# Register loads a block ahead, late sums behind the gelu, a later router and moved bias copies in a fused MoE and recurrent kernel

## The chip, the cores and the metric

The kernel runs on one core of a Trainium2 chip. The metric is the device time of one execution in microseconds (us). Before the change three runs gave 2498.42, 2498.41 and 2495.82 us, median 2498.41. The engines are named as the profile names them: PE is TensorE's matmul stream, PEld its weight loads, DVE is VectorE, ACT is ScalarE, POOL is GpSimd, SP is SyncE (which here only issues DMAs). PEq, DVEq, ACTq and so on are the sequencers of these engines: register operations, register loads, branches and DMA issues run there.

## What is computed

The reference puts two layers one behind the other over 32 sequences of 128 tokens with 512 features, all in float32. Cut to its core:

```python
# layer 0, mixture of 8 small experts, two for each token, and a shared expert
shared = (silu(x @ sw1.T) * (x @ sw3.T)) @ sw2.T
s      = sigmoid(x @ router_w.T + (cond @ router_t_w.T)[:, None, :])
top2   = top_k(s + router_bias, 2)            # gates: s of the two, normalised
routed = sum over the two of gate * (gelu(x @ rw1[e].T) @ rw2[e].T)
h0     = (shared + routed) / 3
# one of 8 large experts for each whole sequence, chosen by its last token
sel    = argmax(softmax(gelu(h0[:, -1] @ Wp1 + bp1) @ Wp2 + bp2))
x      = x + h0 + 0.3 * ((gelu(h0 @ W1[sel] + b1[sel]) @ W2[sel] + b2[sel]) @ Wo + bo)
# layer 1, 16 experts chosen by a hash of the token, with a capacity; then a recurrence
y      = sigmoid(xr @ w_recept.T) * (square(relu(expert_in @ w_key)) @ w_value)[slot]
c      = sigmoid(y@wf.T + c@uf.T + bf) * c + sigmoid(y@wi.T + ...) * tanh(y@wc.T + ...)
x      = x + tanh(y @ wo.T + c_final @ uo.T + bo)
```

## The kernel before

Each float32 operand of a large matmul is cut into a high part (a cast to a reduced float32, on ACT, L64) and the remainder (a subtraction, on DVE, L65); `split` does this, and `mm3` (L82) makes three matmuls of each pair of pieces: high by high, high by low, low by high. So every tile that a matmul reads goes through ACT and then DVE.

The work comes in stages. The 32 sequences are 8 groups of 4 (512 tokens each).

1. **Shared expert, groups 0 to 3** (to about 303 us). `shared` runs over 8 chunks of hidden features for each group: two times 12 matmuls up (`p`), and 12 down into four accumulators (`acc`), a chunk behind. One chunk takes some 10 us at the start. `hook2` puts small work between the chunks. In group 0, `mid0` also spreads the *router* through the chunks: for each group and each of four feature pieces, `fetch_r` loads a piece of x (`xr`), and `router` splits it and adds two matmuls to the scores `rt`, which lie in the only buffer of the PSUM pool `ps_r`; after four pieces ACT copies them to `zt` (L397). `cut` says which pieces belong to which half chunk. The raw pieces of the router, of x and of the weights share one pool of six buffers, and all are loaded over SP's queue. `seq_bias` makes the part of the scores that belongs to the sequence (`ps_tb`): four products on DVE, each then summed over the partitions by a float32 matmul of 256 columns. Its call stands under `if n + w == 1`, which is true for chunk 0, second half, and for chunk 1, first half. After that, `choose` makes the two experts of each token, the list of tokens of each *block* (`blk_t`), the expert of each block (`blk_e`, as a column offset into the weights) and the number of blocks in use (`used_i`). `slots` does the like for layer 1.

2. **Routed experts** (303 to 548 us). A block is 128 token slots of one expert; there are 64 blocks that are always full enough to run and up to seven more (64 to 70). The loop over `i` does for one block: `r_up` (12 matmuls `pur` with the weights at a column that a register holds, then a gelu on ACT into `ge`), `turn_x` for block i+1 (four transposes `ptx`, then the split into `xb`), `take` for block i+3 (POOL's gather), `r_down` for block i-1 (6 matmuls `por` with a register's column, a copy on DVE, a store over SP), and `turn_h` (2 transposes `pth` and a split into `hbr`). The register is loaded by `first_col` (L663) on TensorE, inside `r_up`, and pinned behind the last `pur` of the block before. The blocks beyond 64 come in pairs inside the loop, `maybe` (L702): their registers are loaded first, and then a branch on `used` decides whether they run; `used` is loaded into registers of four engines at i = 12 (L728).

3. **Shared expert, groups 4 to 7**, with the *sums* of the tokens' shared and routed parts between the chunks: `get_o` (two gathers on POOL, L777, and loads of `shc` and `xc` over SP, L784 and L787) and `combine` (two DVE operations, L793 and L794, four transposes `pth`, an ACT scale, stores).

4. **The large expert by sequence** (about 827 to 1430 us). The loop over `b` runs for one sequence at a time: `up` ("a" and "b" halves), `bend` (transposes, gelu with a bias, split into `hb`), `down` (`po`), and for pairs of sequences the output product `pb` and the mixes of layer 1. `used()` splits the next weights, which come by gathers on POOL (`fetch_w`, L906). The biases of the gelu come from `bias_d`, a copy in DRAM that three small-piece DMAs make (L770); the text has them behind the routed blocks, but the scheduler has SP issue them at 3.6, 17.5 and 18.1 us. The sums of the last four sequences, 28 to 31, are done inside this loop: `get_o` at b = 3, 6, 9, 12, `combine` two steps later, and `policy` at b = 17.

5. **Layer 1's experts** (`phD`, `poD`), and 6. **the recurrence** with the output (`ps_f`, `ps_i`, `ps_c`, `poF`) run to the end.

What sets the order: each engine runs its instructions in one order, but this order is not the text's. The compiler's scheduler orders the instructions of all engines by its own estimate, and may move those that depend on nothing unfinished ahead. `tc.issue_after(x)` forbids it to put what stands under it ahead of instruction `x`, and `behind(both)` does that for two instructions. DMA issues take their place in the order of the engine that issues them.

Of the kernel before, what the change touches and what calls it, by code (L numbers as in the profile page):

```python
# [49 lines left out]
def tile_kernel(ctx: ExitStack, tc: tile.TileContext, a: dict, out: bass.AP):  # L50
# [107 lines left out]
    with ExitStack() as sa:  # L158
# [6 lines left out]
        def fetch(src, name):  # L165
            t = raw_p.tile([P, D], F32, tag="raw", name=name)
            nc.sync.dma_start(out=t, in_=src)
            return t

# [35 lines left out]
        def fetch_x(g):  # L205
            if g < NG:
                x_raw[g] = [fetch(a["x"][g][:, k, :], f"xraw_{g}_{k}") for k in range(KD)]
# [68 lines left out]
        with ExitStack() as s0:  # L276
# [32 lines left out]
            fetch_sw(1)  # L309
            ps_acc = s0.enter_context(tc.tile_pool(name="ps_acc0", bufs=4, space=PSUM, **kw))  # L310
# [51 lines left out]
            def seq_bias():  # L362

                ps = ps_r.tile([P, NB, E0], F32, tag="r", name="ps_tb")
                for k in range(KD):
                    pr = rtile([P, NB, E0], f"pr_{k}")
                    nc.vector.tensor_tensor(
                        pr,
                        condT[:, k, :].unsqueeze(2).to_broadcast([P, NB, E0]),
                        rtw[:, k, :].unsqueeze(1).to_broadcast([P, NB, E0]),  # L370
                        ALU.mult,
                    )
                    mm(ps, ones, pr, k == 0, k == KD - 1)
                nc.vector.tensor_copy(tbias, ps)
# [3 lines left out]
            def fetch_r(i):  # L378
                g, k = divmod(i, KD)
                if 0 < g < NG:  # L380
                    xrs[i] = fetch(a["x"][g][:, k, :], f"xr_{g}_{k}")
# [211 lines left out]
            def cut(m):  # L593
                return min(NR, KD + (NR - KD) * (m - 1) // 15) if m > 0 else 0

            def mid0(n, w):

                if n < KF:
                    m = 2 * n + w
                    for i in range(cut(m), cut(m + 1)):  # L600
                        router(i)
                    for i in range(cut(m + 1), cut(m + 2)):
                        fetch_r(i)
                    if n + w == 1:
                        seq_bias()
# [3 lines left out]
            def hook2(g, c):  # L609

                if g == 0:
                    next(steps[0], None)
                    return
                if g == 1 or (g == 2 and c < 5):
                    for _ in range(1):
                        if next(steps[0], 0) == 0:
                            next(steps[1], None)
                    if g == 2 and c == 4:
                        for st in steps:
                            for _ in st:  # L620
# [34 lines left out]
        with s1:  # L655
# [9 lines left out]
            def r_up(i, e=None):  # L665
                if e is None:
                    with tc.issue_after(last_up[0]) if last_up else nullcontext():
                        e = first_col(i)
                x = xb.pop(i)
# [30 lines left out]
            def maybe(n):  # L700
                es = [first_col(i) for i in pairs[n]]
                with tc.If(used > pairs[n][0]):  # L702
                    for i, e in zip(pairs[n], es):
                        r_up(i, e)
# [8 lines left out]

            for i in range(NFULL + 1):
                if i < NFULL:
                    r_up(i)
                    if i + 1 < NFULL:
                        turn_x(i + 1, bx, "xb")
# [4 lines left out]
                if i < NFULL:  # L723
                    turn_h(i)
                n, step = divmod(i - FIRST, STEP)
                if i == FIRST - 4:
                    engines = (nc.tensor, nc.scalar, nc.vector, nc.sync)
                    used = nc.values_load(  # L728
                        used_i[0:1, 0:1], engines=[x.engine for x in engines], min_val=NFULL, max_val=NBLK
                    )  # L730
# [38 lines left out]
        for kind, i in BIAS.items():  # L769
            nc.sync.dma_start(out=bias_d[:, bass.ts(i, KD)], in_=a[kind][:, KD * D :])  # L770
# [127 lines left out]
        raws, bcol, changed = {}, {}, {}  # L898
# [3 lines left out]
        def fetch_w(i):  # L902
            if i < len(todo):
                kind, b = order[todo[i]]
                raws[i] = wg.tile([P, WROW], F32, tag="raw", name=f"rawB_{i}")
                nc.gpsimd.indirect_dma_start(  # L906
# [3 lines left out]
                )  # L910
                if kind == "W1a":
# [95 lines left out]
    with ExitStack() as sb:  # L1007
# [35 lines left out]
        seqs, end_p = {}, None  # L1043
# [17 lines left out]
        def fetch_hid(b):  # L1061
            if b < NB:
                hid_raw[b] = lp.tile([P, KD, P], F32, tag="hid", name=f"hidB_{b}")
                nc.sync.dma_start(out=hid_raw[b].rearrange("p k q -> p (k q)"), in_=by_seq(hid_d, b))
# [156 lines left out]
        for b in range(-1, NB + 1):  # L1221
            c, j = divmod(b - 1, PB)
            if b + 1 < NB:
# [3 lines left out]
                fetch_hid(b + 3)  # L1227
            gated = b - 4 if b % 2 == 0 and 0 <= b - 4 < NB - 6 else None
# [555 lines left out]
```

## Time and profile before

The profiled execution took 2497.2 us; its span, from the first to the last instruction that the profile shows, is 2495.5 us.

| What | Value | Where it is read |
|---|---|---|
| median of three runs | 2498.41 us (2495.82 to 2498.42) | the times |
| profiled execution, span | 2497.2 us, 2495.5 us | the times, the page's head |
| mean granted TensorE clock | 0.991 | clock of the core |
| first matmul | at 6.46 us | timeline |
| PE busy in 0 to 50 us | 39.28 of 50.00 us | busy time by windows |
| PE busy in 303 to 548 us | 236.08 of 245.00 us, clock 0.99 | busy time by windows |
| PE busy in 820 to 850 us | 23.34 of 30.00 us, clock 0.89 | busy time by windows |
| DMA from SP's queue | 246.51 MB, 29.9% of 16 engines | queues |

How to read it: a row of the timeline gives start, duration, engine, line, operation, output and inputs, and in brackets how long the engine had been idle and who ended the idle time. In the list of waits the columns are the total, the number of times and the longest wait, in us. Rows marked PEq or PEldq are the sequencer's, not the matrix unit's. The ends of matmuls are modelled, so that a matmul's row overlaps the next; distances between starts are the safer measure.

### The profile page before, as it was taken

What the parts mean: (1) busy time and instruction counts of PE and PEld (TensorE: products, weight loads), DVE (VectorE), ACT (ScalarE), POOL (GpSimd) and SP (SyncE); (2) the same over time, 40 slices, a digit from 0 to 9 for tenths busy, and PEclk for the clock granted to TensorE, in tenths of its full rate; (3) what the DMA queues carried; (4) which work ended last, traced back from release to release, by engine and by line L of the source; (5) the groups of instructions that cost most, each with busy time, mean ns of one, the idle gap of its engine ahead of it and who ended that gap; (6) DMA issues with size and microseconds to landing.
All of it is one profiled execution on the core that took longest, in us unless ns stands there. A gap on an engine that the chain in (4) does not pass through costs nothing.

```text
span 2495.5 us, 36566 instructions
## 1 busy us (share of the span) xinstructions
PE 2434.5 (98%) x12932; PEld 2060.7 (83%) x12932; DVE 1326.8 (53%) x2265; ACT 1034.5 (41%) x1826; POOL 412.3 (17%) x462
## 2 busy tenths in 40 slices
PE   8999999999999899999999999999999999999996
PEld 5788888888888788888888889999978888888885
DVE  7897644456567344454454486766642333333336
ACT  4444533343224454454454376666532222222214
POOL 1000022221233233322222100000010000000003
PEclk9999999999999999999999999999999999999998
DMA  5545544457564333341342487777431111111017
GB/s 181 168 126 169 187 161 161 163 185 238 183 215 165 115 120 127 102 153 57 118 146 94 152 295 232 222 228 234 155 125 39 38 40 42 43 42 38 26 70 280
DMA packets 193402, 351.62 MB, mean 141 GB/s; under 512 B 37504, under 2 KB 72368, under 8 KB 190144
## 3 DMA queue, kind: packets, MB, share of 16 engines
q1 hardware_dynamic: 142080, 246.51, 29.9%
q0 software_dynamic: 36448, 75.95, 10.3%
q10 hardware_dynamic: 14688, 26.75, 3.0%
q8 instruction: 108, 1.77, 0.3%
q14 instruction: 78, 0.64, 0.1%
HBM read 373.94 MB, written 88.65 MB: 185 GB/s over the span
## 4 chain that ended last, share of the span: by engine, by line
PE 49%; DVE 2%; DMA 1%; ACT 0%; issue 0%; POOL 0%; SPq 0%; POOLq 0%; DVEq 0%; ACTq 0%
PE phD L82 7%; PE ps_c L82 7%; PE ps_f L82 7%; PE ps_i L82 7%; PE poD L82 7%; PE poF L82 3%; PE po L82 3%; PE pb L82 2%; PE pv L82 1%; PE ptF L1481 1%; PE ptC L1488 1%; PE ptD L1348 0%; DMA v_d<-r 0%; DMA rawD<-in_w_value_dram 0%; PE ptB L1196 0%
## 5 line engine op out<-in xcount | busy, mean ns | idle before, releaser
L65 DVE TENSOR_TENSOR wD<-rawD,wD 128x1024 fp32r<-128x1024 f32 x128 | 156.4, 1229 | 80.8 <-ACT wD L64 80.7
L82 PE MATMUL p<-xhl,swu 128*128 128x512 f32 x768 | 188.7, 397 | 6.5 <-ACT xhl L64 6.5
L82 PE MATMUL phD<-xe,wD 128*128 128x256 f32 x1536 | 186.9, 282 | 2.0 <-DVE hf L1367 2.0
L82 PEld LDWEIGHTS phD<-xe,wD 128*128 128x128 f32 x1536 | 186.0, 190 | 3.3 <-issue 2.2
L82 PE MATMUL p<-xhl,kept_u 128*128 128x512 f32 x768 | 184.3, 394 | 0.7 <-DVE kept_u L65 0.7
L82 PE MATMUL poD<-wD,hD 128*128 128x512 f32 x768 | 181.3, 392 | 0.0
L82 PEld LDWEIGHTS p<-xhl,swu 128*128 128x128 f32 x768 | 144.6, 190 | 36.9 <-ACT xhl L64 6.5
L82 PEld LDWEIGHTS p<-xhl,kept_u 128*128 128x128 f32 x768 | 141.9, 188 | 30.0 <-DVE kept_u L65 1.1
L82 PEld LDWEIGHTS poD<-wD,hD 128*128 128x128 f32 x768 | 142.0, 188 | 28.4
L64 ACT CAST wD<-rawD 128x1024 fp32r<-128x1024 f32 x128 | 133.2, 1047 | 55.4 <-PE poD L82 50.1
L281 POOL DMA_INDIRECT xg<-in_x_rows_dram,blk_t x71 | 67.6, 952 | 454.9 <-PE ptx L291 246.4
L1456 POOL DMA_INDIRECT y<-res_d,gat_i x32 | 30.8, 962 | 573.6 <-DVE r L1476 492.1
L82 PE MATMUL pur<-r,xb 128*128 x792 | 111.5, 291 | 7.2 <-issue 4.2
L82 PE MATMUL por<-r,hbr 128*128 x396 | 108.0, 407 | 1.2 <-ACT hbr L64 1.2
L82 PEld LDWEIGHTS pur<-r,xb 128*128 128x128 f32 x792 | 99.7, 192 | 9.0 <-issue 6.9
L65 DVE TENSOR_TENSOR xb<-ptx,xb 128x512 fp32r<-128x512 f32 x68 | 47.0, 691 | 106.4 <-ACT xb L64 104.7
L82 PE MATMUL poF<-z,wo_hl 128*128 128x512 f32 x384 | 96.4, 399 | 0.0
L82 PE MATMUL ps_f<-wf_hl,z 128*128 128x512 f32 x384 | 96.2, 399 | 0.0
L82 PE MATMUL ps_c<-wc_hl,z 128*128 128x512 f32 x384 | 94.7, 396 | 0.7 <-ACT z L64 0.7
L82 PE MATMUL pb<-rT,Wo_hl 128*128 128x256 f32 x768 | 94.7, 281 | 0.3 <-DVE rT L65 0.2
L82 PE MATMUL acc<-swd,as 128*128 128x512 f32 x384 | 95.0, 392 | 0.0
L82 PE MATMUL pv<-w_recept_hl,xr 128*128 128x512 f32 x384 | 93.1, 391 | 0.5 <-ACTq L934 0.4
(1017 smaller groups left out, 4955.6 us busy)
## 6 DMA issues: line engine op xcount, KB each, us to landing
rawD<-in_w_key_dram SPq DMA_DIRECT2D x64, 512.0 KB, 4.3
rawD<-in_w_value_dram SPq DMA_DIRECT2D x64, 512.0 KB, 4.4
swr<-in_sw_dram SPq DMA_DIRECT2D x120, 256.0 KB, 3.2
o_d<-obr SPq DMA_DIRECT2D x66, 256.0 KB, 2.4
xraw<-in_x_dram SPq DMA_DIRECT2D x32, 256.0 KB, 4.2
rraw<-in_rw_dram SPq DMA_DIRECT2D x32, 256.0 KB, 3.0
xc<-in_x_dram SPq DMA_DIRECT2D x32, 256.0 KB, 3.5
hid_d<-o ACTq DMA_DIRECT2D x32, 256.0 KB, 2.2
```

Source lines behind the costliest of these rows:

```text
L64: first = nc.scalar.copy(hi, src).ins
L65: done = nc.vector.tensor_tensor(lo, src, hi.bitcast(F32), ALU.subtract).ins
L82: done = nc.tensor.matmul(ps, lhsT=left(hl, k), rhs=right(hr, k), start=start and k + n == 0, stop=stop and 3 * k + n == last,)
L281: nc.gpsimd.indirect_dma_start(out=xg[i], out_offset=None, in_=a["x_rows"], in_offset=bass.IndirectOffsetOnAxis(ap=blk_t[:, i : i + 1], ax ...
L1456: got = nc.gpsimd.indirect_dma_start(out=y, out_offset=None, in_=res_d, in_offset=bass.IndirectOffsetOnAxis(ap=gat_i[:, b : b + 1], axis=0),)
L1481: nc.tensor.transpose(pt[:, k, :], r[:, bass.ts(k, P)], ident)
L1488: nc.tensor.transpose(pt[:, k, :], c[:, bass.ts(k, P)], ident)
```

## The change

The change has five parts.

- **Router and start.** In group 0, the even pieces of x are loaded over ACT's queue. The router's later pieces get their own six buffers (`xrr`) and are pinned behind the first loads. `cut` begins two half chunks later and ends at the same place. `seq_bias` is called once, behind the last chunk of group 0; the four products are added up on DVE and one matmul sums over the partitions.
- **Bias copies.** The three copies into `bias_d` are issued in group 1, one behind each of the chunks 0, 2 and 4, pinned behind the load that was issued last.
- **Columns ahead.** `know(i + 1)` loads the column register of the next block right behind `r_up(i)`, pinned behind its last matmul; `r_up` only takes the register. The registers of the blocks in pairs are loaded in the same place, some blocks ahead of the pair, and no longer in `maybe`. At i = 13 the load is pinned behind TensorE's load of `used`, and `turn_h` behind ACT's and DVE's.
- **`used`.** Its loads are pinned behind the last `pur` and the last split.
- **Late sums.** For sequences 28 to 31 `get_o` is pinned behind the last load of `hid` and the last weight gather, and `combine` and `policy` come behind `bend` and are pinned behind its split.

```diff
-        def fetch(src, name):
+        def fetch(src, name, queue=nc.sync):
             t = raw_p.tile([P, D], F32, tag="raw", name=name)
-            nc.sync.dma_start(out=t, in_=src)
+            last_load[:] = [queue.dma_start(out=t, in_=src).ins]
             return t
...
-                x_raw[g] = [fetch(a["x"][g][:, k, :], f"xraw_{g}_{k}") for k in range(KD)]
+                x_raw[g] = [
+                    fetch(a["x"][g][:, k, :], f"xraw_{g}_{k}", nc.scalar if g == 0 and k % 2 == 0 else nc.sync)
+                    for k in range(KD)
+                ]
...
             fetch_sw(1)
+            first_loads = last_load[0]
...
-                ps = ps_r.tile([P, NB, E0], F32, tag="r", name="ps_tb")
+                sum_ = None
                 for k in range(KD):
...
-                    mm(ps, ones, pr, k == 0, k == KD - 1)
+                    if k > 0:
+                        nc.vector.tensor_tensor(pr, pr, sum_, ALU.add)
+                    sum_ = pr
+                ps = ps_r.tile([P, NB, E0], F32, tag="r", name="ps_tb")
+                mm(ps, ones, sum_, True, True)
...
-                    xrs[i] = fetch(a["x"][g][:, k, :], f"xr_{g}_{k}")
+                    xrs[i] = rt.tile([P, GT], F32, tag="xrr", bufs=6, name=f"xr_{g}_{k}")
+                    with tc.issue_after(first_loads):
+                        nc.sync.dma_start(out=xrs[i], in_=a["x"][g][:, k, :])
...
-                return min(NR, KD + (NR - KD) * (m - 1) // 15) if m > 0 else 0
+                return min(NR, KD + (NR - KD) * (m - 3) // 13) if m > 2 else 0
...
-                    for i in range(cut(m + 1), cut(m + 2)):
+                    for i in range(cut(m + 2), cut(m + 3)):
                         fetch_r(i)
-                    if n + w == 1:
-                        seq_bias()
...
                     next(steps[0], None)
+                    if c == KF - 1:
+                        seq_bias()
                     return
+                if g == 1 and c % 2 == 0 and c < 6:
+                    kind = list(BIAS)[c // 2]
+                    with tc.issue_after(last_load[0]):
+                        nc.sync.dma_start(out=bias_d[:, bass.ts(BIAS[kind], KD)], in_=a[kind][:, KD * D :])
...
-            def r_up(i, e=None):
-                if e is None:
+            cols = {}
+
+            def know(i):
+
+                if i < NBLK:
                     with tc.issue_after(last_up[0]) if last_up else nullcontext():
-                        e = first_col(i)
-                x = xb.pop(i)
+                        cols[i] = first_col(i)
+
+            def r_up(i):
+                x, e = xb.pop(i), cols.pop(i)
...
             def maybe(n):
-                es = [first_col(i) for i in pairs[n]]
                 with tc.If(used > pairs[n][0]):
-                    for i, e in zip(pairs[n], es):
-                        r_up(i, e)
+                    for i in pairs[n]:
+                        r_up(i)
...
+            know(0)
             for i in range(NFULL + 1):
+                n, step = divmod(i - FIRST, STEP)
                 if i < NFULL:
                     r_up(i)
                     if i + 1 < NFULL:
+                        with tc.issue_after(loads[0]) if i == FIRST - 3 else nullcontext():
+                            know(i + 1)
+
+                        if -3 <= i - FIRST and n + 1 < len(pairs) - 1 and step in (3, 4):
+                            for q in pairs[n + 1][step - 3 : step - 2]:
+                                know(q)
                         turn_x(i + 1, bx, "xb")
...
                 if i < NFULL:
-                    turn_h(i)
-                n, step = divmod(i - FIRST, STEP)
+                    with behind(loads[1:3]) if i == FIRST - 3 else nullcontext():
+                        turn_h(i)
                 if i == FIRST - 4:
...
-                    used = nc.values_load(
-                        used_i[0:1, 0:1], engines=[x.engine for x in engines], min_val=NFULL, max_val=NBLK
-                    )
+                    with tc.issue_after(last_up[0]), behind(last_split):
+                        used = nc.values_load(
+                            used_i[0:1, 0:1], engines=[x.engine for x in engines], min_val=NFULL, max_val=NBLK
+                        )
...
-        for kind, i in BIAS.items():
-            nc.sync.dma_start(out=bias_d[:, bass.ts(i, KD)], in_=a[kind][:, KD * D :])
...
+            late, step = divmod(b - 3, 3)
+            if 0 <= late < GB and step == 0:
+                with tc.issue_after(last_hid[0]), tc.issue_after(last_w[0]):
+                    get_o(NB - GB + late, cb, 1)
...
-            late, step = divmod(b - 3, 3)
-            if 0 <= late < GB and step == 0:
-                get_o(NB - GB + late, cb, 1)
-            if 0 <= late < GB and step == 2:
-                combine(NB - GB + late, ps_t)
-            if late == GB and step == 2:
-                policy(PARTS[0], NB, cb, ps_t)
             if b + 1 < NB:
                 bend(b + 1, "a")
+            with behind(last_split):
+                if 0 <= late < GB and step == 2:
+                    combine(NB - GB + late, ps_t)
+                if late == GB and step == 2:
+                    policy(PARTS[0], NB, cb, ps_t)
```

`last_w` and `last_hid` hold the last weight gather and the last load of `hid`.

More of the change, by code (lines that the diff above doesn't have):

```diff
@@ L163, in tile_kernel @@
         xgp = sxg.enter_context(tc.tile_pool(name="xgp", bufs=3, **kw))
-        def fetch(src, name):
+        def fetch(src, name, queue=nc.sync):
             t = raw_p.tile([P, D], F32, tag="raw", name=name)
-            nc.sync.dma_start(out=t, in_=src)
+            last_load[:] = [queue.dma_start(out=t, in_=src).ins]
             return t
+        last_load = []
         NSW = KF * NG
@@ L723, in tile_kernel @@
                 if i < NFULL:
-                    turn_h(i)
-                n, step = divmod(i - FIRST, STEP)
+                    with behind(loads[1:3]) if i == FIRST - 3 else nullcontext():
+                        turn_h(i)
                 if i == FIRST - 4:
                     engines = (nc.tensor, nc.scalar, nc.vector, nc.sync)
-                    used = nc.values_load(
-                        used_i[0:1, 0:1], engines=[x.engine for x in engines], min_val=NFULL, max_val=NBLK
-                    )
+                    with tc.issue_after(last_up[0]), behind(last_split):
+                        used = nc.values_load(
+                            used_i[0:1, 0:1], engines=[x.engine for x in engines], min_val=NFULL, max_val=NBLK
+                        )
+                    loads = [
+                        next(x for x in reversed(nc.cur_bb.bb.instructions) if x.engine == e.engine)
+                        for e in engines
+                    ]
                 if FIRST - 6 <= i < FIRST - 4:
@@ L897, in tile_kernel @@
         ws = {}
-        raws, bcol, changed = {}, {}, {}
+        raws, bcol, changed, last_w = {}, {}, {}, []
         todo = [0, 1, 3, 2, *range(4, len(order))]
@@ L905, in fetch_w @@
                 raws[i] = wg.tile([P, WROW], F32, tag="raw", name=f"rawB_{i}")
-                nc.gpsimd.indirect_dma_start(
+                got = nc.gpsimd.indirect_dma_start(
                     out=raws[i], out_offset=None, in_=a[kind],
@@ L910, in fetch_w @@
                 )
+                last_w[:] = [got.ins]
                 if kind == "W1a":
@@ L1041, in weight_b @@
             return pair
-        seqs, end_p = {}, None
+        seqs, end_p, last_hid = {}, None, []
         def seq(p, queue=nc.sync):
@@ L1063, in fetch_hid @@
                 hid_raw[b] = lp.tile([P, KD, P], F32, tag="hid", name=f"hidB_{b}")
-                nc.sync.dma_start(out=hid_raw[b].rearrange("p k q -> p (k q)"), in_=by_seq(hid_d, b))
+                last_hid[:] = [
+                    nc.sync.dma_start(out=hid_raw[b].rearrange("p k q -> p (k q)"), in_=by_seq(hid_d, b)).ins
+                ]
         def by_seq(t, p):
```

## The prediction

> **What bounds the kernel now.** I read the busy shares first, then TensorE's own waits, then three places on the timeline, with the sequencer's rows and the granted clock beside them.
>
> ```profile
> PE 2434.5 (98%) x12932; PEld 2060.7 (83%) x12932; DVE 1326.8 (53%) x2265; ACT 1034.5 (41%) x1826; POOL 412.3 (17%) x462
> ```
>
> TensorE sets the time: 2434.5 of 2495.5 us, the next engine 53%. So an edit is worth the TensorE work that it takes away, and the TensorE idle time that it takes away or makes. The list of who TensorE waits for (total, times, longest, in us) says where idle time is:
>
> ```profile
> PE po L82 <- DVE hb_0a L65: 6.7, 1, 6.7
> PE p L82 <- ACT xhl L64: 6.5, 1, 6.5
> PE pur L82 <- issue: 4.2, 1, 4.2
> ...
> PE pur L82 <- PEq L702: 1.9, 1, 1.9
> PE rt L56 <- DVE rwa L359: 1.8, 1, 1.8
> PE ps_tb L56 <- ACT zt L397: 1.7, 1, 1.7
> ...
> PE ps_tb L56 <- DVE tbias L374: 0.8, 1, 0.8
> ```
>
> Every one of these lies where the change works. Two of the stalls are followed by a second cost. In these windows the columns are us, PE, PEld, DVE, ACT and POOL busy, then the granted clock:
>
> ```profile
> 369.20:373.90 4.70, 4.63 (x22) 4.64 (x23) 0.00 (x0) 0.38 (x1) 0.00 (x0) 0.51 0.00 0
> ...
> 844.00:848.30 4.30, 4.30 (x10) 3.36 (x11) 1.24 (x2) 0.00 (x0) 2.19 (x3) 0.50 0.31 106
> ```
>
> TensorE came back from 4.2 and 6.7 us of idleness at half clock, for 4.7 and 4.3 us: about 2.3 and 2.1 us more lost.
>
> **The routed blocks, the part that decides.** From 303 to 548 us one block follows another every 3.43 us: 12 matmuls `pur`, 4 transposes `ptx` for the next block, 6 matmuls `por`, 2 transposes `pth`:
>
> ```profile
> 449.17 0.60 PE L291 MATMUL ptx<-ident,xg 128*128 128x128 f32 x4
> 449.37 0.38 ACT L675 ACTIVATE ge<-pur 128x256 f32<-128x256 f32 x1 [1.01 <-PE pur L82]
> ...
> 449.80 0.59 ACT L64 CAST xb<-ptx 128x512 fp32r<-128x512 f32 x1
> ...
> 450.42 0.69 DVE L65 TENSOR_TENSOR xb<-ptx,xb 128x512 fp32r<-128x512 f32 x1 [1.60 <-ACT xb L64]
> ...
> 451.13 1.64 PE L82 MATMUL pur<-r,xb 128*128 x12
> ...
> 452.61 0.60 PE L291 MATMUL ptx<-ident,xg 128*128 128x128 f32 x4
> ```
>
> What the page doesn't count as busy is TensorE's sequencer. Each `pur` and `por` has an address computed from a register (FUSED_REGOPS, L82), and each block one load of that register (TENSOR_LOAD, L663). The rows of those lines in three stretches (449.5 to 450.9, 451.12 to 452.55, 361 to 371 us), with the first and last start:
>
> ```profile
> L663 PEldq TENSOR_LOAD <-blk_e x1: 444/444/444, 449.8 to 449.8; - x1
> ...
> L82 PEldq FUSED_REGOPS  x9: 46/46/46, 451.2 to 452.3; - x9
> ...
> L663 PEldq TENSOR_LOAD <-blk_e x7: 297/304/523, 363.5 to 367.9; - x7
> ```
>
> Three things are to be seen. First, a load with its range check holds the sequencer (367.9 - 363.5) / 6 = 0.73 us, and seven in a row starve TensorE: that is the 4.2 us. Second, the sequencer does not run past a matmul that waits. The load at 449.8 stands behind `pth`, which waits for the gelu, and the gelu ends at 449.37 + 0.38 = 449.75. Three of the twelve `pur` addresses are done early; the third `pur` waits for `xb`, which DVE ends at 450.42 + 0.69 = 451.11, and the other nine addresses run from 451.2 to 452.3, one per (452.3 - 451.2) / 8 = 0.14 us. Third, by then the sequencer is hardly ahead: its last address is at 452.3 and `ptx` starts at 452.61. Today the load stands after `pth` and ahead of `pur`. There the six `por` (1.64 us) are already queued and hide it: blocks of 3.43 us show no idle time.
>
> The change issues the load for block i+1 right behind the `pur` of block i; in the compiled order it stands between `pur` and `ptx` in 61 places. So after the address at 452.3 comes the load at about 452.4, and `ptx` can be handed over at about 452.4 + 0.73 = 453.1 instead of 452.61. The `por` behind it are late by as much, and so is the next `xb`, which starts when `ptx` ends and ends 1.35 us later: nothing is won back within the block, and no engine has slack to give, since `xb` releases the next `pur`. Bounds of the unseen stall: 0 if the sequencer gains its lead somewhere I don't see, 0.73 if nothing overlaps. I take 0.5, the row's own arithmetic: 61 x 0.5 = +30.5 us.
>
> The page "Perfetto Trace Analysis" of the Trainium skill ("Tensor Engine Instruction") has a waiting matmul stand in a wait queue while the sequencer is already free for the next instruction. By that rule the load would slip under the twelve `pur` and cost nothing, and the sum would be rival 1's. The rows above contradict it for these matmuls, so I follow the rows.
>
> The loads for the seven blocks beyond 64 move from clusters to second loads in the same place, which nothing hides: 7 x 0.73 = +5.1, and `used` (L728) is a further load ahead of one `ptx`, +0.7. What goes: the first cluster, 4.2 us of which about 0.5 stays for the branch (two later branches with no cluster cost about that), -3.7, and its half clock, -2.3; the two loads ahead of the second branch (L702, 1.9 us), -1.4. The block loop: 30.5 + 5.1 + 0.7 - 7.4 = **+28.9 us** (bounds -7.4 and +42.9).
>
> **The late sums.** The 6.7 us come from DVE's order:
>
> ```profile
> 841.63 0.75 DVE L793 SCALAR_TENSOR_TENSOR o<-o,g,shc 128x512 f32<-128x512 f32 x1 [10.02 <-DMA shc<-sh_d]
> ...
> 843.26 0.68 DVE L65 TENSOR_TENSOR hb_0a<-hf_0a,hb_0a 128x512 fp32r<-128x512 f32 x1
> ```
>
> A sum of group 7 waits for its load (`shc`, issued on SP at 832.4 behind the loads of Wo), and the gelu's lower half `hb_0a` stands behind it, although its input was done at 834.8. Pinned behind the gelu's split, and fetched from the fourth block on, the sum has nothing behind it that TensorE wants: -6.7, and the half clock after it -2.1. Later sums cost TensorE 0.8 + 0.6 + 0.5 us near 929 (a transpose and its two successors); half of that may go, -0.9 (0 to -2). The gathers and `shc`/`xc` loads move behind the weights' and `hid`'s in POOL's and SP's queues, so those come earlier; the sums have two blocks, some 36 us, to arrive. Together **-9.7 us** (-7 to -11).
>
> **The start.** `seq_bias` ran twice with four matmuls in two passes each:
>
> ```profile
> 28.73 1.97 PE L56 MATMUL ps_tb<-pr,ones 128*128 128x256 f32 x8 [1.66 <-ACT zt L397]
> ...
> 32.20 1.99 PE L56 MATMUL ps_tb<-pr,ones 128*128 128x256 f32 x8 [0.81 <-DVE tbias L374]
> ```
>
> From the start of each to the next matmul (30.35, 33.85) is 1.6 us. One matmul remains, a quarter of one run: 2 x 1.6 - 0.4 = -2.9. Its waits (1.7 + 0.8) go, and `rwa`'s 1.8 should halve because five more matmuls stand ahead: -3.4. DVE loses four products of 0.41 us and gains three sums, hidden at 53% busy. Half of group 0's x goes over ACT's queue: the first matmul waits until 6.46 us for `xhl`, perhaps 1 us less, which at the clock of the first 12 us (matmuls 0.43 us apart instead of 0.23) is worth half: -0.5 (0.5 to -1.5). Two DMA issues stand ahead of ACT's table load, which ends at 2.1 us, and its first split starts at 3.6: covered. The router starts a chunk later and then takes 28 pieces in 13 half-chunks instead of 15, with one PSUM bank: each group waits for the last copy (`zt`, 0.57 us). I add +1.5 (0 to +7). The bias copies leave SP's queue, where an `xr` landed 4.0 us late; in group 1 each holds SP for 0.5 to 0.7 us while weights are a chunk (10 us) ahead: 0. Without that cover it is 2 us. The start: -2.9 - 3.4 - 0.5 + 1.5 = **-5.3 us** (-9 to +1).
>
> **Sum.** 28.9 - 9.7 - 5.3 = +13.9. Against the profiled execution's own time, 2497.2 (span 2495.5 and 1.7 around it), this is 2511.1 us; the median shown is 2498.4, 1.2 above. I say **2511 us**.
>
> **Rivals.** (1) The load is hidden where it is put: slots, second loads and `used` cost 0, all gains stay: 2497.2 - 7.4 - 9.7 - 5.3 = **2474.8**, faster. For it: at 305.5 us a load stood behind `pur` and cost nothing. Against: those twelve addresses had been computed under earlier matmuls, without the wait for `xb`. It decides if the sequencer is 0.73 us ahead at the last `pur`; the row says 0.3. (2) Half hidden: 0.25 per slot and half for the others, 15.3 + 2.9 - 7.4 - 15.0 = -4.2: **2493**, on the edge between faster and no change. It would need `xb` 0.25 us earlier; ACT's part already starts when `ptx` ends. (3) The router's crowding eats the start: copies and late `xr` stall TensorE at each of seven groups for about 1 us: **2517**. For it: 0.3 us waits on `zt` and `xrhl` exist; against: DVE and ACT have room. (4) The load costs all of 0.73: 14 more, **2525**.
>
> **Chances.** Forecast 0.60 (its own range 2503 to 2517), rival 1 0.14, rival 2 0.10, rival 3 0.10, rival 4 0.06. The range 2493 to 2519 leaves out rivals 1 and 4. What a measurement can tell from no change is about 0.2%, 5 us. Faster: rival 1 and half of rival 2 less a little, 0.18; same: the rest of rival 2 and the forecast's tail, 0.09; slower 0.73.
>
> **What would show it.** In the later profile: blocks 3.9 us apart, with idle time on `ptx` of about 0.5 us (waiting for issue or the sequencer) 61 times; the stretch of routed blocks 29 us longer; `pur` without 4.2 and 1.9; no half clock after either stall; `po` without the wait for `hb_0a`; `ps_tb` x2 instead of x16. I am wrong if blocks stay at 3.43 us with the load in its new place: then the sequencer does run past waiting matmuls.

## The result, and the profile after

The changed kernel takes 2516.36 us (median of 4 runs, 2514.71 to 2520.32), the kernel before 2498.41 us beside it (4 runs, 2495.82 to 2499.13): a ratio of 1.0076, 95% interval 1.0059 to 1.0093. It is slower by 0.8%. The profiled run took 2515.7 us, with a span of 2514.0.

The busy shares of the changed kernel say almost nothing of it; TensorE's busy time is 3 us longer, the rest of the loss is idle time:

```profile
PE 2437.2 (97%) x12918; PEld 2056.4 (82%) x12918; DVE 1324.7 (53%) x2263; ACT 1034.3 (41%) x1826; POOL 414.9 (17%) x462
```

The list of who TensorE waits for in the changed kernel (total us, times, longest us) answers to the one of before:

```profile
PE ptx L296 <- PE pur L82: 19.2, 48, 0.7
PE ptx L296 <- issue: 10.6, 11, 1.7
PE pth L828 <- DVE o L825: 7.2, 5, 3.6
PE p L82 <- ACT xhl L64: 6.3, 1, 6.3
...
PE rt L56 <- DVE rwa L365: 1.1, 1, 1.1
```

Gone are `po` for `hb_0a` (6.7), `pur` for issue (4.2) and for the queue at the branch (1.9), and `ps_tb` (1.7 and 0.8). New are the two lines on `ptx`, 59 times and 29.8 us. The 0.8 us that `pth` waited for `o` have become 7.2.

To see which stage each part of the change moved, take the first start of a few matmuls as marks. All kernels of this study, in us: `ps_z` turns the router's scores at the end of group 0; "routed" is from the first `pur` to the first product of the kept shared weights, where the shared experts of groups 4 to 7 begin; the two columns after it are stretches of the large expert by sequence (`pu_6a` is the first product of sequence 6); "time" is the profiled run:

| kernel | first `ps_z` at | first `pur` at | routed | `pu_0a` to first `po` of `hb_0b` | `pu_6a` to `pu_19a` | time |
|---|---|---|---|---|---|---|
| before | 108.9 | 305.4 | 243.1 | 24.0 | 238.3 | 2497.2 |
| after | 100.2 | 296.7 | 275.2 | 15.1 | 246.7 | 2515.7 |
| cols_undone | 99.4 | 298.2 | 244.5 | 15.1 | 244.9 | 2487.3 |
| two_loads | 99.3 | 297.8 | 335.3 | 15.6 | 246.7 | 2585.5 |
| after_ptx | 99.6 | 297.7 | 250.3 | 15.1 | 245.0 | 2492.5 |
| late_old_place | 100.0 | 298.2 | 275.1 | 15.1 | 238.3 | 2515.7 |
| late_alone | 109.9 | 310.1 | 246.4 | 15.1 | 245.1 | 2500.1 |
| seq_bias_only | 110.1 | 308.9 | 246.4 | 23.2 | 238.3 | 2501.3 |
| xr_own | 106.1 | 304.9 | 245.7 | 24.4 | 238.3 | 2497.6 |
| router_late | 104.2 | 304.9 | 247.0 | 24.0 | 238.3 | 2498.6 |
| start_alone | 100.1 | 299.2 | 243.9 | 24.2 | 238.3 | 2491.0 |
| x_one_queue | 98.9 | 297.0 | 246.6 | 23.5 | 238.5 | 2493.7 |
| best1 | 100.2 | 299.1 | 242.1 | 15.1 | 237.8 | 2480.0 |

Between before and after the start gains 8.7 us, the routed blocks lose 32.1, the stall ahead of `hb_0b` gives 8.9 and the later sums take 8.4 back; the rest of the span gives 4.5 (1.1 of it in the shared experts, 3.4 behind `pu_19a`). Sum: +18.4, and the spans differ by 18.5.

A caution on the table: stretches that no edit touched differ between runs, too. The shared experts behind the routed blocks took 278.0 to 283.8 us in kernels with the same instructions there. The routed blocks with their loads in the old place took 243.1 to 247.0 us in eight kernels, and the first `pur` behind the start of before came at 305.4 and at 310.1 us. The kernel before, run beside the experiments, took 2500.5, 2502.8 (median of 11) and 2497.5 us. All experiments but the last have one run each. So the verdicts below go by the stretch that an edit touches, and no difference below about 4 us is read in the whole time.

Two blocks in the timeline of the changed kernel (start, duration, engine, line, operation; in brackets the idle time before it and what ended it):

```profile
439.74 1.63 PE L82 MATMUL pur<-r,xb 128*128 x12
441.76 0.63 PE L296 MATMUL ptx<-ident,xg 128*128 128x128 f32 x4 [0.39 <-PE pur L82]
442.14 1.65 PE L82 MATMUL por<-r,hbr 128*128 x6
442.43 0.59 ACT L64 CAST xb<-ptx 128x512 fp32r<-128x512 f32 x1 [0.57 <-PE ptx L296]
443.04 0.69 DVE L65 TENSOR_TENSOR xb<-ptx,xb 128x512 fp32r<-128x512 f32 x1 [2.19 <-ACT xb L64]
443.63 0.38 PE L703 MATMUL pth<-ident,ge 128*128 128x128 f32 x2
443.77 1.63 PE L82 MATMUL pur<-r,xb 128*128 x12
445.73 0.63 PE L296 MATMUL ptx<-ident,xg 128*128 128x128 f32 x4 [0.33 <-PE pur L82]
```

And the sequencer's rows of the load's line in the first of them:

```profile
L679 PEldq TENSOR_LOAD <-blk_e x1: 296/296/296, 441.0 to 441.0; - x1
L679 PEldq FUSED_REGOPS  x1: 151/151/151, 441.4 to 441.4; - x1
L679 PEldq SEQ_ASSERT  x1: 18/18/18, 441.6 to 441.6; - x1
```

The load starts while the last `pur` are running, its range check ends after 441.6, and `ptx` starts at 441.76, 2.02 us after the block's first `pur`. Before it was 1.48 (451.13 to 452.61). The block is 443.77 - 439.74 = 4.03 us long instead of 3.43, and the split that makes the next `xb` ends at 443.73, again just ahead of the next block's first `pur`: nothing was won back.

### The profile page after: what moved, and what is told of

Read it like the earlier page. It is cut to its first block, busy times and chain, and to the rows that moved or that the text cites. A ratio compares the mean times of both kernels' runs of the same rounds, so it can differ in the third digit from the quotient of the medians.

```text
span 2514.0 us, 36524 instructions
## 1 busy us (share of the span) xinstructions
PE 2437.2 (97%) x12918; PEld 2056.4 (82%) x12918; DVE 1324.7 (53%) x2263; ACT 1034.3 (41%) x1826; POOL 414.9 (17%) x462
## 4 chain that ended last, share of the span: by engine, by line
PE 53%; DVE 2%; DMA 2%; ACT 1%; issue 0%; POOL 0%; SPq 0%; POOLq 0%; DVEq 0%; ACTq 0%
PE ps_f L82 7%; PE ps_c L82 7%; PE ps_i L82 7%; PE poD L82 7%; PE phD L82 6%; PE po L82 4%; PE poF L82 3%; PE pb L82 2%; PE pv L82 2%; PE ptF L1517 1%; PE ptC L1524 1%; DMA r<-v_d 0%; PE ptD L1384 0%; PE ptB L1230 0%; DMA v_d<-r 0%
## 5 line engine op out<-in xcount | busy, mean ns | idle before, releaser
L82 PE MATMUL ps_i<-wi_hl,z 128*128 128x512 f32 x384 | 93.0, 391 | 0.0
```

Of the source, the lines that this page charges most:

```text
L82: done = nc.tensor.matmul(ps, lhsT=left(hl, k), rhs=right(hr, k), start=start and k + n == 0, stop=stop and 3 * k + n == last,)
```

## The experiments

**The columns put back.** The register loads and the loads of `used` as in the kernel before; the start and the late sums as changed. Part of the edit:

```diff
-            know(0)
             for i in range(NFULL + 1):
...
-                            know(i + 1)
...
-                x, e = xb.pop(i), cols.pop(i)
+                if e is None:
+                    with tc.issue_after(last_up[0]) if last_up else nullcontext():
+                        e = first_col(i)
+                x = xb.pop(i)
```

> The changed kernel with the routed blocks' columns loaded as before: each load behind the transposes of the gelu and ahead of its own block's matmuls, clusters in front of the branches. Theory (the load behind the 12 pur stalls TensorE): the stretch from the first pur to the first product of the kept shared weights goes back from 275.2 to about 243.1 us, and the whole from 2515.7 to about 2484 us (32 less); no idle time on ptx. Rival (the routed stretch is longer because of something that the start moved into it, the blocks' gathers or the later router): the stretch stays near 275 us and the time near 2515 us.

Routed 244.5 us, the time 2487.3, against 2500.5 for the kernel before beside it. No `ptx` wait is left but 0.4 us at a branch; the stalls of the clusters are back:

```profile
PE pur L82 <- issue: 5.0, 2, 4.2
...
PE pur L82 <- PEq L718: 1.9, 1, 1.9
```

The 31 us of the routed stretch belong to this part of the change, and without it the change is a gain. That it is the place of the column loads, and not the pins of `used` that go with them, the next two kernels show.

**Two loads for one.**

```diff
                     with tc.issue_after(last_up[0]) if last_up else nullcontext():
+                        first_col(i)
                         cols[i] = first_col(i)
```

> The changed kernel with every column loaded twice at its new place (one more register load with its range check behind the 12 pur; the result is not changed by it). Theory (the sequencer's time for the load is what delays ptx, and nothing overlaps a second one): 0.73 us per block, about 68 of them in this stretch, so the stretch of routed blocks is 275 + 50 = 325 us, a block 4.7 us, the time about 2565 us (2560 to 2567). Rival (ptx is late for another reason, by its order against xb or by the wait for the blocks' rows): a second load costs nothing, 2516 us. A middle rival (0.5 us for any load there): 34 more, 2550 us.

Routed 335.3 us: 60.1 more for 71 more loads, 0.85 us each on the average. Timeline of TensorE, and two of the sequencer's rows in the first of these blocks:

```profile
374.19 1.63 PE L82 MATMUL pur<-r,xb 128*128 x12
377.15 0.63 PE L296 MATMUL ptx<-ident,xg 128*128 128x128 f32 x4 [1.32 <-issue]
377.54 1.63 PE L82 MATMUL por<-r,hbr 128*128 x6
379.01 0.38 PE L704 MATMUL pth<-ident,ge 128*128 128x128 f32 x2
379.14 1.63 PE L82 MATMUL pur<-r,xb 128*128 x12
```

```profile
L679 PEldq TENSOR_LOAD <-blk_e x2: 309/442/574, 375.4 to 376.1; - x2
L679 PEldq SEQ_ASSERT  x2: 18/18/18, 376.0 to 377.0; - x2
```

`ptx` now starts 2.96 us after the block's first `pur`: 1.48 without a load, 2.02 with one, 2.92 with two in the median block. The first load with its check holds the sequencer for 0.69 us (the median here, and of the single loads in the changed kernel), the second for 0.92: its TENSOR_LOAD takes 574 ns in this block where the first takes 309 (0.53 and 0.30 us in the medians). So about 0.15 us of the first load is hidden under the last `pur`, of the second nothing. The theory was right that nothing overlaps a second load; its price of 0.73 fits a single load and is too low for a second one behind it. The rivals of nothing and of 0.5 are out.

**The load behind the transposes.**

```diff
-                            know(i + 1)
...
                         turn_x(i + 1, bx, "xb")
+                            know(i + 1)
```

`know` is pinned behind the last `ptx` in place of the last `pur`.

> The changed kernel with the next block's load moved by one place, from in front of the four transposes ptx to just behind them, still a block ahead. Theory (the place decides: what stands behind the load is late by what the sequencer has no lead for, and ptx starts the chain to the next xb): por is late by about 0.2 us instead of ptx by 0.5; a block takes 3.6 to 3.7 us, the routed stretch 252 to 258 us, the time 2493 to 2499 us. Rival (loading a block ahead costs about 0.5 us a block wherever it stands): 4.0 us a block, 2515 us. Second rival (the load is hidden entirely): 3.43 us a block, 2484 us.

Routed 250.3 us, the time 2492.5: better than the theory's 252 to 258, more of the load is hidden than I gave it. One place further on, the same load, just as far ahead, costs 3 to 7 us more than the old place with its clusters (243.1 to 247.0 in the table), instead of 28 to 32. In the timeline, for a while, every second block pays 0.3 us and the others nothing:

```profile
312.12 1.66 PE L82 MATMUL pur<-r,xb 128*128 x12
313.62 0.60 PE L298 MATMUL ptx<-ident,xg 128*128 128x128 f32 x4
314.22 1.68 PE L82 MATMUL por<-r,hbr 128*128 x6
315.74 0.38 PE L705 MATMUL pth<-ident,ge 128*128 128x128 f32 x2
315.87 1.66 PE L82 MATMUL pur<-r,xb 128*128 x12
317.37 0.60 PE L298 MATMUL ptx<-ident,xg 128*128 128x128 f32 x4
317.73 1.62 PE L82 MATMUL por<-r,hbr 128*128 x6
```

From `ptx` to `por` it is 0.60 us in the first block and 0.36 in the second; the blocks are 3.75 and 3.45 us long. The load starts 1.31 us after the block's first `pur` in the first and 1.05 us in the second, where the split of `xb` had ended 0.30 us before that `pur`: a block that comes late finds its `xb` ready, its addresses run earlier, and the load is covered. This alternation was read, not tested.

**The late sums back in their place.** Sums and policy ahead of the next gelu again; their loads stay late.

```diff
+            if 0 <= late < GB and step == 2:
+                combine(NB - GB + late, ps_t)
...
             if b + 1 < NB:
                 bend(b + 1, "a")
-            with behind(last_split):
-                if 0 <= late < GB and step == 2:
-                    combine(NB - GB + late, ps_t)
```

> The changed kernel with the late sums and the policy issued ahead of the first gelu of the next block again, not behind its split; their loads stay where the change put them. Theory (pinned behind the split, the second sum stands on VectorE behind the split of the weights, 2.35 us a half, and its transposes, which stand in the middle of po on TensorE, wait 3.6 and 2.2 us with a half clock after each): from pu_6a to pu_19a 246.7 goes back to 239 to 241 us, no wait of pth for o above 1 us, the time about 2509 us. The stall in front of hb_0a does not come back, since the loads are still later. Rival (the later loads, not the place of the sums, make the waits): 246 us as now, 2515 us.

From `pu_6a` to `pu_19a` it is 238.3 us, as before the change, and the stretch ahead of `hb_0b` stays at 15.1. The whole time did not follow (2515.7, 2509 expected): the first `pur` came 1.5 us later, the shared experts took 281.5 us instead of 278.0, and the rest behind `pu_19a` 3.4 us longer. These 8.4 us lie in stretches that this edit doesn't touch, and eat the whole gain. In the changed kernel VectorE's order makes the stall; its timeline, with TensorE's transposes among it:

```profile
944.90 0.69 DVE L65 TENSOR_TENSOR hb_6a<-hf_6a,hb_6a 128x512 fp32r<-128x512 f32 x1 [1.26 <-ACT hb_6a L64]
945.51 0.75 DVE L824 SCALAR_TENSOR_TENSOR o<-o,g,shc 128x512 f32<-128x512 f32 x1
946.17 2.36 DVE L65 TENSOR_TENSOR wB_W1b<-rawB,wB_W1b 128x1024 fp32r<-128x1024 f32 x2
948.44 0.49 DVE L1216 SCALAR_TENSOR_TENSOR dx<-dx,maa_r_sb,x 128x256 f32<-128x256 f32 x1
948.84 0.75 DVE L825 SCALAR_TENSOR_TENSOR o<-o,g,o 128x512 f32<-128x512 f32 x1
949.50 1.28 DVE L1216 SCALAR_TENSOR_TENSOR dx<-dx,maa_r_sb,x 128x256 f32<-128x256 f32 x3
949.74 0.63 PE L828 MATMUL pth<-ident,o 128*128 128x128 f32 x4 [3.59 <-DVE o L825]
```

The pin holds the first of the sum's two operations behind the gelu's split (`hb_6a`); two slices of a weight's split (2.36 us for both) and one of `dx` fall between it and the second. The sum's transposes stand in TensorE's order in the middle of `po`, and TensorE waits 3.59 us for them. With the sums in their old place no wait of `pth` for `o` that would show in the list is left in this stretch.

**The late sums alone.** The kernel before with that part of the change.

> The kernel before with the part of the late sums alone. Theory (the pin trades one stall for others): the stretch from pu_0a to the first po of hb_0b falls from 24.0 to 15.1 us, and that from pu_6a to pu_19a rises from 238.3 to about 246 us, since the second sum stands on VectorE behind the weights' split: 2496 to 2498 us, no gain. Rival (the 8.4 us there come from the router's or the columns' part of the change, in loads or in code): 238 us, the time 2488 us.

15.1 and 245.1 us: the theory's pair. The part gains 8.9 and gives 6.8 back by itself, so the loss needs neither the router nor the columns. The 1.6 us up to the 246.7 of the changed kernel fit a half clock: the waits of 3.6 and 2.2 us are in both kernels, but only in the changed one is the second of them, too, followed by 3.4 us at half clock (the last section shows it). Of the other kernels with the sums pinned, `two_loads` has both half clocks and 246.7 us, `cols_undone` and `after_ptx` have one and 244.9 and 245.0. The time, 2500.1 us, shows no gain, as the theory had it (2496 to 2498).

**The start in pieces.** Five kernels, all without the columns' and the late sums' parts. First `seq_bias` alone:

```diff
+                    if k > 0:
+                        nc.vector.tensor_tensor(pr, pr, sum_, ALU.add)
+                    sum_ = pr
...
-                    if n + w == 1:
-                        seq_bias()
...
+                    if c == KF - 1:
+                        seq_bias()
```

> The kernel before with one part of the start: seq_bias runs once, at the end of group 0, with its four products summed on VectorE and one matmul; the router, the loads of x and the bias copies are as before. Of the 8.7 us that group 0 became shorter than before (102.5 to 93.8 us between the first matmul and ps_z), the prediction gave 5.4 to this part (2.9 of matmuls and 2.5 of its waits). Theory as predicted: group 0 97 us long, so about 3 us of the 8.7 come from the later router. Rival (the waits round seq_bias were the whole of it, the rt wait for rwa and the router's among them): 94 us. Second rival (the waits move to the router's next pieces): 100 us or more. Time 2489 to 2495 us.

Group 0 ends at 110.1 us, and the first `pur` comes at 308.9, against 310.1 in `late_alone` and 305.4 in the profile before, which have the start of before: no gain that shows. From the first matmul, group 0 takes 105.2 us, the second rival's case, and the time is 2501.3 us, not 2489 to 2495. The 14 matmuls are gone, the waits are not:

```profile
PE rt L56 <- DVE rwa L359: 3.6, 1, 3.6
PE rt L56 <- ACT xrhl L64: 1.6, 2, 1.2
PE rt L56 <- ACT zt L401: 1.2, 2, 0.9
```

A half clock follows the first of them; the columns of this windows view are us, PE, PEld, DVE, ACT and POOL busy, and the granted clock:

```profile
20.50:25.80 5.30, 5.09 (x12) 2.45 (x13) 3.84 (x12) 1.71 (x3) 0.00 (x0) 0.50 0.34 71
```

Then the later router alone, and its loads alone (buffers of their own, issued behind the first weights):

```diff
-                    xrs[i] = fetch(a["x"][g][:, k, :], f"xr_{g}_{k}")
+                    xrs[i] = rt.tile([P, GT], F32, tag="xrr", bufs=6, name=f"xr_{g}_{k}")
+                    with tc.issue_after(first_loads):
+                        nc.sync.dma_start(out=xrs[i], in_=a["x"][g][:, k, :])
...
-                return min(NR, KD + (NR - KD) * (m - 1) // 15) if m > 0 else 0
+                return min(NR, KD + (NR - KD) * (m - 3) // 13) if m > 2 else 0
```

`xr_own` has the first hunk, `router_late` both.

> The kernel before with the later router alone: its pieces start with the third half-chunk and take 13 of them, and its loads xr have buffers of their own and follow the first weights; seq_bias still runs twice with four matmuls each, x comes over one queue. Marks to compare: the first pur starts at 305.4, 310.1 and 308.9 us in runs with the router as before, at 296.7 to 299.2 us in runs with the whole start. Theory (what the start gained is the later router: TensorE no longer waits for rwa and the xr): first pur at 299 to 303 us, the wait for rwa below 1.5 us; time about 2494 us. Rival (seq_bias and the router gain only together, since the 14 matmuls and their waits move elsewhere when one is left): 305 us or more, 2500 us. The prediction had this part at a loss of 1.5 us.

> The kernel before with one half of that part: the loads xr have buffers of their own and are issued behind the first weights; the router's pieces stand where they were. Theory (the loads' order decides: xr took the place of weights in the queue and the buffers): first pur at 301 to 303 us, the wait for rwa near 1 us. Rival (the place of the router's matmuls decides, with five more matmuls ahead of the first rt): 306 to 310 us, the wait for rwa 1.8 to 3.6 us as before.

Both have the first `pur` at 304.9 us: `router_late` at the edge of its rival, `xr_own` between theory and rival. Their times, 2498.6 and 2497.6 us against 2497.5 for the kernel before beside them, show no gain. `xr_own` still waits 2.5 us for `rwa`; in `router_late` that wait is gone, and the one left is made by `seq_bias`:

```profile
PE ps_tb L56 <- DVE pr L370: 1.8, 1, 1.8
```

The whole start, and the whole start with x on one queue:

> The kernel before with the parts of the start alone (x of group 0 over two queues, seq_bias once, the router later, the bias copies in the second group). If the parts add up: group 0 94 us long instead of 102.5, 2 to 3 us more at the loads of the end of the block phase, nothing in the routed blocks (243 to 244.5 us) and nothing in the late sums: 2497.2 - 8.7 - 2 = about 2487 us (2484 to 2490). Rival (the gain of the start is given back where the weights' loads and the router meet the next groups): group 0 short, the stretch to the first pur longer by as much, 2494 us or more.

> The kernel with the whole start alone (first matmul at 6.5 us, first pur at 299.2 us), but with x of group 0 on one queue as before. In the runs so far the first matmul starts at 6.5, 5.5 and 4.9 us with one queue and at 6.3 to 6.9 us with two. Theory (the second queue does not bring x earlier, it lets the weights and x share the same engines): first matmul at 4.9 to 6.5 us, first pur within 1 us of 299.2 or earlier. Rival (the second queue brings the first matmul about 1 us earlier, as the prediction put it): first matmul at 7 us or later, first pur later by up to 1.5 us.

`start_alone` has group 0 at 100.1 us and the first `pur` at 299.2: its gain is not given back. Its 2491.0 us (2502.8 before beside it) lie 1 us above the theory's 2484 to 2490. With x on one queue (98.9 and 297.0 us) it is no worse: the first matmul starts at 6.0 us instead of 6.5, and the wait for `rwa` is 0.2 us. So no gain from the second queue shows. The page "Trainium Kernel Development and Optimization" of the Trainium skill ("Key Constraints") has it that loads from several queues run on the same 16 DMA engines and interleave, and that several queues save issue time only; the first matmuls of these runs, 4.9 to 6.5 us with one queue and 6.3 to 6.9 with two, agree in so far as the second queue brought x no earlier; no run here shows the interleaving itself.

The parts of the start do not simply add up. Against the two kernels with the start of before (first `pur` at 305.4 and 310.1 us), `seq_bias` alone is between 3.5 us worse and 1.2 better, the later router alone 0.5 to 5.2 better, and the whole start, in eight kernels (one of them with x on one queue), 6.2 to 13.4 better (296.7 to 299.2 us). Whichever of the two one measures from, the whole is worth at least 4.5 us more than the two single gains added up. With the router done, the rest is worth 5.7 to 7.9 us (304.9 to 299.2 and 297.0), and the trace of `router_late` shows most of it: 2.8 us of extra matmuls of `seq_bias` and the 1.8 us that they wait.

One rival is left. `seq_bias_only`, `router_late` and `xr_own` still issue the bias copies at the start (at 3.6 us, and two more between 17 and 31 us), and the kernels with the whole start issue them from about 90 us on. No kernel moves the copies alone, so what the whole start has over its two parts may in part be theirs.

**A version with the load in a covered place.** The columns are loaded two blocks ahead, behind the transposes of the gelu, where the load stood before the change; a block beyond 64 has its column loaded between `por` and these transposes. The loads of `used` are pinned behind these transposes, too. The late sums stand ahead of the next gelu, the policy behind its split. Part of the edit:

```diff
+            know(1)
...
-                            know(i + 1)
...
+                                    know(q, last_down)
                         turn_h(i)
+                    if i + 2 < NFULL:
+                        know(i + 2)
```

> The changed kernel with two places altered: the columns are loaded two blocks ahead, behind the transposes of the gelu (where the load stood before), and a block of the second sort has its column loaded between por and these transposes; and the late sums are issued ahead of the next gelu again, while the policy stays pinned behind its split. Theory (the load's place decides, not how far ahead it is; the sums' place makes the 8.4 us): blocks of 3.43 us, no clusters in front of the branches, routed stretch 237 to 240 us; pu_6a to pu_19a 238 to 239 us; start as in the changed kernel: 2473 to 2478 us, faster than both. Rival (a load two blocks ahead, or one that stands between por and pth, costs about 0.5 us a block as well): routed stretch 270 us or more, 2507 us.

2480.62 us (median of 6 runs) against 2502.77 for the kernel before beside it (11 runs): a ratio of 0.9914, 95% interval 0.9899 to 0.9929. It beats the kernel before, by less than the whole time that the theory gave (2473 to 2478). The timeline:

```profile
446.54 1.63 PE L82 MATMUL pur<-r,xb 128*128 x12
448.01 0.60 PE L296 MATMUL ptx<-ident,xg 128*128 128x128 f32 x4
448.37 1.64 PE L82 MATMUL por<-r,hbr 128*128 x6
449.84 0.38 PE L703 MATMUL pth<-ident,ge 128*128 128x128 f32 x2
449.98 1.29 PE L82 MATMUL pur<-r,xb 128*128 x9
```

Its load starts at 448.7 us (413 ns, then the check) while six `por` are queued, and the block is 449.98 - 446.54 = 3.44 us long. A load two blocks ahead is as cheap as one block ahead, in this place. Where two loads stand in one block, the block takes 3.7 to 4.7 us, so the routed stretch comes to 242.1 us, not 237 to 240. That is 1 to 5 us less than the old place with its clusters (243.1 to 247.0); how much of the clusters' cost came back, one profile does not tell more closely.

## Why the prediction came out as it did

**The routed blocks: right.** +28.9 us were forecast and 32.1 came (30.6 between `late_old_place` and `cols_undone`). The named signs are there: blocks of 4.0 us (3.9 forecast) and idle time on `ptx`, 0.40 us in 48 cases. The arithmetic behind the stall, a load of 0.73 against a lead of 0.3, was off in one number, the lead: a single load holds the sequencer for 0.69 us there and delays `ptx` by 0.54, so only about 0.15 is hidden. The difference of the forecast's own two numbers is 0.43; the 0.5 that was taken lies closer. The cluster's own stalls went, as forecast, and blocks with two loads take 4.8 to 5.4 us.

**The rivals of a hidden or half hidden load: out.** `two_loads` shows the price, `after_ptx` and `best1` that the same load is cheap one place on and free where six `por` cover it. By the page "Perfetto Trace Analysis" of the Trainium skill ("Tensor Engine Instruction"), read as the prediction read it, the load would have slipped under the waiting `pur`; in 59 places here it did not.

**The late sums: half right, and its second half is the step that failed.** The 6.7 us and their half clock went: 8.9 against 8.8 forecast. But the forecast went on: "the sum has nothing behind it that TensorE wants", and half of the later waits would go, -0.9. In fact they rose, by 8.4 us in that stretch. Behind the sum's first operation stand the weights' split and then the sum's second operation, and the sum's own transposes are what TensorE wants: they stand in the middle of `po`. Moving the sums back removes exactly these 8.4 us (`late_old_place`), and that part of the change alone makes 6.8 of them (`late_alone`); the rest fits the second half clock. So the term was -9.7 (-7 to -11) and came to about -0.5.

**The start: the sum undersized, for a wrong term.** -5.3 were forecast, -8.7 came, inside the bounds (-9 to +1). The forecast gave 6.3 of gain to `seq_bias` and the wait for `rwa` (2.9 + 3.4) and charged the later router 1.5. Run alone, the router cost nothing: the first `pur` came 0.5 to 5.2 us earlier. So the failed term here is the router's: the loss did not show, and a gain of some size did. `seq_bias` alone returned none of its gain that shows, and in `router_late` its extra matmuls and their wait are the 4.6 us that are left to win (2.8 + 1.8): the gain is there once the router is out of the way. How much of the whole belongs to the moved bias copies, which the forecast put at 0, stays open. The crowding of the router that was priced (and made rival 3) did not show: behind its first matmul, the changed kernel waits in group 0 1.1 us for `rwa` and for nothing else in the list. The half us for x over two queues was not there either (6.3 us against 6.5 in the two profiles, and the other way round in `x_one_queue`).

**The total** was 5 us low: +13.9 forecast, +18.5 measured, made of +3.2 in the routed blocks, +9.2 in the late sums, -3.4 at the start and -4.5 in stretches that the forecast left at nothing. The routed blocks carry the sign by themselves. That the size came out so close is luck: with the other terms as forecast, the late sums alone would have put the time at 2520 us, above the stated 2519, and the start and the untouched stretches happened to take most of it back.

**Left open.** Why stretches with the same instructions, such as the shared experts, differ by up to 6 us between kernels (in six of them TensorE waits there 1.4 to 1.9 us for the policy's `pl`, and in the others not, which may be a part of it); whether the 1.8 us wait for `rwa` in the profile before, against 3.5 in `late_alone` with the same start and 3.6 in `seq_bias_only`, is the order of the loads or their speed; and what the bias copies cost at the start.

## What to carry to other kernels

A register load on a busy engine is priced by what stands behind it, not by how far ahead of its use it is: put it where work already queued covers it, and not ahead of the instruction that starts the longest chain (here `ptx`, from which the next `xb` is made). When an operation is pinned behind another, pin its second half too, and look for its consumers in every other engine's order: a consumer in the middle of a chain stalls that chain. Parts that each remove a wait are tried together as well as alone, since one wait can hide another.

## What the hardware showed that was not expected

**The price of a load.** One register load with its check kept TensorE's sequencer for 0.73 us on the average in a row of seven in the profile before, and for 0.69 us in the median alone in its new place. A second load right behind it there took 0.92 us in the median (`two_loads`), because its TENSOR_LOAD took 0.53 us instead of 0.30; why, no run shows.

**A half clock after short stalls.** The changed kernel runs at half clock for 3.4 us after TensorE waited only 2.22 us for the second late sum:

```profile
1118.20:1121.60 3.40, 1.18 (x7) 0.71 (x6) 3.40 (x5) 1.69 (x3) 0.26 (x1) 1.00 0.00 0
1121.60:1125.00 3.40, 3.40 (x12) 2.72 (x11) 1.39 (x5) 0.75 (x2) 1.35 (x3) 0.50 0.48 77
```

In the stretch before the half clock TensorE was still busy for 1.18 of 3.40 us. The page "TensorE: Matmul & The Clock Gate" of the Trainium skill ("Part 1: The HAM clock gate") asks for at least one idle window of about 3.4 us; here a stretch of that length with a third of it busy was enough. It does not always follow. The same wait of 2.22 us in `cols_undone` leaves the clock full:

```profile
1090.40:1093.90 3.50, 1.28 (x7) 0.77 (x5) 3.50 (x5) 1.99 (x3) 0.06 (x1) 1.00 0.00 0
1093.90:1097.30 3.40, 3.40 (x24) 3.10 (x25) 1.59 (x5) 1.97 (x6) 1.58 (x3) 1.00 0.41 46
```

Every wait of 3.3 us or more behind the first matmul was followed by a half clock, in all thirteen kernels. Of the shorter ones some were (1.8 us on `pl` in `best1`, 2.5 on `rt` in `xr_own`) and some were not (1.8 us on `rt` in the profile before, 2.6 on `ptC` in `late_alone`), so in this range the length of the wait does not decide. Two half clocks followed no wait at all: in `after_ptx`, TensorE was busy for all of 99.4 to 102.9 us, in 39 short matmuls, and then ran at 0.50 to 106.3; in `late_alone` the same happened at 113.3 us. What decides is open.
